# A four-layer graph network on one core: the kernel computes the issue order of its engines itself

## The chip, the cores and the metric

The kernel runs on one core of a Trainium2 chip. A core has five engines, each with its own queue of instructions that it works through in order: TensorE (PE in the profile; its weight loads are listed as PEld), VectorE (DVE), ScalarE (ACT), GpSimd (POOL) and SyncE (SP, which here only issues transfers). Engines wait for each other by semaphores. The metric is device time of one execution in microseconds. The page and the views come from one profiled execution; the times of the runs come from executions without the profiler.

## The reference

There are 16 graphs of 1024 nodes with 256 features, each with a dense 0/1 adjacency. Four layers follow each other, each on a normalized and rectified copy of x, and each adds its output to x:

```python
h = jnp.maximum(_layernorm(x), 0.0); x = x + layer0(h, adj)
# layer 0: e = leaky_relu(f1[i] + f2[j], 0.2), softmax over axis 1 where adj > 0, attention @ (h W), elu
# layer 1: the same, with softmax over the last axis
# layer 2: relu(x W_upd + (adj^T (x W_msg)) / degree + bias)
# layer 3: four heads of 64 features, leaky_relu with 0.01, softmax, relu(attention @ h + bias) + h,
#          then a layernorm over each head's 64 features with gamma and beta
```

All data are fp32, and the products are computed in fp32 (layer 2's message product in two fp32r halves, hi and lo).

## The kernel before

The 1024 nodes of a graph are eight tiles of 128. For each graph, `graph(b)` (a Python generator) traces: a `Norm` (statistics, normalization on ACT into `hn`, L671, transposition on TensorE into `pt_h`, L684, copy to `ht`, L685), then the four layers. A layer projects the eight tiles (`project`, L690), turns one projected column into a row that lies on all 128 partitions (`spread` writes `d_row` to HBM, L709; `everywhere` reads it back to every partition as `row`, L715), builds eight tiles of unnormalized weights `p` of 128 x 1024 on DVE (layer 0 L800 and L802, layer 1 L861, layer 3 L968, once per head) and multiplies them with the projected features on TensorE (L790, L854, L981; layer 2 multiplies the adjacency itself, L922, after its update product, L916). `residual` (L759, L760) adds the output to x on DVE and starts the next layer's `Norm`.

Layer 3's products (L981) are half as wide as the others: two matmuls of 64 columns each use the two halves of the array (`128*64` in the profile); all others use `128*128`. A matmul of fp32 is two records in the profile.

Graphs overlap. Each generator yields a number after each piece, a planned duration, and a small queue at the end of `tile_simple_stack` always resumes the generator with the earliest planned time; the next graph starts 120 planned microseconds after the one before. So the traced order interleaves layer 3 of a graph with layers 0 and 1 of the next. The traced order is not the issued one: the Tile scheduler takes the traced instructions, simulates them, and puts each engine's queue in the order in which they became ready, the earlier traced first. It also gives each tile one of its pool's slots. A tile's `tag` names its pool of slots and `bufs` their number: `p` has 8, `p3` (layer 3's `p`) 5, `hn` 3, and `e`, `v` and the PSUM tags `tr`, `mm`, `at` and `hd` 2.

`later = tc.keep_in_program_order` pins an instruction behind the one traced before it on its engine. The kernel before uses it for all transfers of SP, for the last DVE instructions of `tail` and for layer 0's early products. POOL issues the loads of x (L547) and of the adjacency's blocks (`load_adj`, L589), and computes the inverse deviations (`inv_std`, L596 and L597).

Of the kernel before, what the change touches and what calls it, by code (L numbers as in the profile page):

```python
# [14 lines left out]
P = 128  # L15
# [404 lines left out]

@with_exitstack
def tile_simple_stack(
# [35 lines left out]
    later = tc.keep_in_program_order  # L458
# [29 lines left out]
    def load_w(src, width, name, total, wait=True):  # L488
        t = const.tile([P, DC, total], F32, name=name)
        if wait:  # L490
            behind(t[:1, 0, :1])
        later(nc.sync.dma_start(t[:, :, :width], src.rearrange("(c p) f -> p c f", p=P)))
        return t
# [3 lines left out]
    def weights01(layer, w, w_t, a, order, wait=True):  # L497

        wx[layer] = t = load_w(w, D, f"wx{layer}", D + 2, wait)
        wts = work.tile([P, N], F32, tag="p3", name="wts", bufs=5)[:, : DC * D].rearrange("p (c f) -> p c f", c=DC)  # L500
        if wait:
            behind(wts[:1, 0, :1])
        later(nc.sync.dma_start(wts, w_t.rearrange("(c p) f -> p c f", p=P)))
        avs = small.tile([P, DC, 2], F32, tag="avs", name="avs", bufs=1)
        later(nc.sync.dma_start(avs, a.rearrange("(c p) k -> p c k", p=P)))
        for fc in range(DC):
            ps = mm_ps.tile([P, HALF], F32, tag="mm", name="ps_wa")
            for ec in range(DC):
                nc.tensor.matmul(
                    ps[:, :2], wts[:, ec, fc * P : (fc + 1) * P], avs[:, ec, :], start=(ec == 0), stop=(ec == DC - 1)  # L510
                )
            for k, to in enumerate(order):
                nc.vector.tensor_copy(t[:, fc, D + to : D + to + 1], ps[:, k : k + 1])

    def weights2():
        wx[2] = t = load_w(w2_msg, D, "wx2", 2 * D)
        later(nc.sync.dma_start(t[:, :, D:], w2_upd.rearrange("(c p) f -> p c f", p=P)))
        for name, src in (("bias2", bias2), ("bias3", bias3), ("gamma3", gamma3), ("beta3", beta3)):
            rows[name] = const.tile([P, D], F32, name=f"row_{name}")
            behind(rows[name][:1, :1])  # L520
            later(nc.sync.dma_start(rows[name], src.partition_broadcast(P)))
# [3 lines left out]
    def weights3():  # L525

        wx[3] = t = load_w(w3, D, "wx3", W3)
        w3ts = work.tile([P, N], F32, tag="p3", name="w3ts", bufs=5)[:HO, :].rearrange("p (h f) -> p h f", h=H)
        behind(w3ts[:1, 0, :1])
        later(nc.sync.dma_start(w3ts, w3_t))  # L530
        a3s = work.tile([P, D], F32, tag="e", name="a3s")[:HO, : H * T2].rearrange("p (h t) -> p h t", h=H)
        later(nc.sync.dma_start(a3s, a3))
        for fc in range(DC):
            for h in range(H):
                ps = mm_ps.tile([P, HALF], F32, tag="mm", name="ps_wa3")
# [4 lines left out]
    def load_x(b):  # L540
        t = state.tile([P, NT, D], F32, tag="xs", name="xs", bufs=3)
# [8 lines left out]
    class Mask:  # L550
# [10 lines left out]
        def load(self):  # L561
# [5 lines left out]
            raw = work.tile([P, HALF], I32, tag="raw", name="raw", bufs=self.AHEAD)  # L567
            later(nc.sync.dma_start(raw, adj_t[self.b, n * P : (n + 1) * P, g * HALF : (g + 1) * HALF]))
            self.raws.append((s, n, g, raw))

        def step(self, count=1):
            if self.bytes is None:
                self.bytes = state.tile([P, NT, N], U8, tag="mask", name="mask")
# [10 lines left out]
    def load_adj(b, g):  # L584

        t = state.tile([P, NT, EIGHTH], F32R, tag="adj", name="adj", bufs=4)
# [6 lines left out]
    def inv_std(var, n, scale, eps):  # L593

        rs = small.tile([P, NT * H], F32, tag="rstd", name="rs", bufs=6)
# [4 lines left out]
    def new_ht():  # L600
        return state.tile([P, DC, N], F32, tag="ht", name="ht", bufs=2)

    class Norm:
# [6 lines left out]
        def __init__(self, times=None):  # L610
            self.ht, self.rs, self.power, self.waiting, self.times, self.due = new_ht(), [], [], None, times, None
            if times is not None:
                self.shifts = small.tile([P, NT], F32, tag="shifts", name="shifts", bufs=2)
                self.scales = small.tile([P, 2, NT], F32, tag="scales", name="scales", bufs=2)
            self.mv = small.tile([P, NT, 2], F32, tag="mv", name="mv", bufs=4)
# [9 lines left out]
        def pair(self, xs, g, sums=None):  # L625

            if self.times is None:
                self.flip()
                shift = small.tile([P, 2], F32, tag="shift", name="shift")
            else:  # L630
                shift = self.shifts[:, 2 * g : 2 * g + 2]
            if sums is None:
                for k in range(2 * g, 2 * g + 2):
                    st = small.tile([P, 6], F32, tag="bn", name="st")
# [32 lines left out]
        def shifted(self, xs, g, by):  # L667
            hns = []
            for k, (scale, bias) in enumerate(by):
                hn = work.tile([P, D], F32, tag="hn", name="hn", bufs=3)  # L670
# [4 lines left out]
        def flip(self):  # L675
# [5 lines left out]
            pt = tr_ps.tile([P, DC, 2 * P], F32, tag="tr", name="pt_h")  # L681
# [5 lines left out]
    def project(norm, w, n, width):  # L687
        ps = mm_ps.tile([P, HALF], F32, tag="mm", name="ps_proj")
# [4 lines left out]
    def new_hs(name="hs"):  # L693
        return state.tile([P, NT, W3], F32, tag="hs", name=name, bufs=3)

    def spread(col, n, scales, name):
# [5 lines left out]
        ps = tr_ps.tile([P, P], F32, tag="tr", name="ps_col")  # L702
        nc.tensor.transpose(ps[:k, :], col, ident)
        all_rows = []
        for scale in scales:
            e = small.tile([H * NT, P], F32, tag="e_row", name="e_row", bufs=2)
            nc.scalar.activation(e[:k, :], ps[:k, :], AF.Exp, scale=scale)
            d = dram.tile([n, N], F32, tag=f"row_{name}", name="d_row", bufs=4)
            later(nc.sync.dma_start(d.rearrange("r (t p) -> (r t) p", p=P), e[:k, :]))  # L709
# [3 lines left out]
    def everywhere(d, tag):  # L713
        row = work.tile([P, N], F32, tag=tag, name="row", bufs=2)
        later(nc.sync.dma_start(row, d.partition_broadcast(P)))  # L715
        return row

    class Row:


        def __init__(self):
            self.ps = [hd_ps.tile([P, HALF], F32, tag="hd", name="ps_row") for _ in range(NHALF)]

        def add(self, n, f):
            g, k = divmod(n, PER)
            diag = work.tile([P, D], F32, tag="e", name="diag")[:, :P]
# [3 lines left out]
        def rows(self, scales):  # L730
            made = [work.tile([P, N], F32, tag="row", name="row", bufs=2) for _ in scales]
# [5 lines left out]
    def column(src, n):  # L737

        col = small.tile([P, H, NT], F32, tag="col", name="col", bufs=2)
# [7 lines left out]
    def weights(name):  # L747
        return work.tile([P, N], F32, tag="p", name=name, bufs=NT)

    def residual(xs, i, v, after, e=None):  # L750

        x = xs[:, i, :]
        if i % 2 == 0:
# [3 lines left out]
            after.sums = small.tile([P, 2], F32, tag="sums", name="sums")  # L757
# [7 lines left out]
    def layer0(b, xs, m, norm, after):  # L765
# [14 lines left out]
        q = small.tile([P, NT], F32, tag="q", name="q")  # L780
# [4 lines left out]
        early = [at_ps.tile([P, HALF], F32, tag="at", name="ps_o0") for _ in range(EARLY)]  # L785
        if b == 0:
            early += [hd_ps.tile([P, HALF], F32, tag="hd", name="ps_o0") for _ in range(NHALF)]

        def product(ps, i, j):
            m = nc.tensor.matmul(  # L790
                ps[:, :D], ps_[j][:, i * P : (i + 1) * P], hs[:, j, :D], start=(j == 0), stop=(j == NT - 1)
            )
            if i < len(early) and j < 7:
                later(m)

        for j in range(NT):
# [4 lines left out]
            z = small.tile([P, 2], F32, tag="z", name="z", bufs=8)  # L801
# [12 lines left out]
        for i in range(NT):  # L814
            if i < len(early):
                ps = early[i]
            else:
                ps = at_ps.tile([P, HALF], F32, tag="at", name="ps_o0")
                for j in range(NT):
                    product(ps, i, j)  # L820
            e = work.tile([P, D], F32, tag="e", name="e")
            nc.scalar.activation(e, ps[:, :D], AF.Exp)  # L822
            v = work.tile([P, D], F32, tag="v", name="v")
# [5 lines left out]
    def layer1(b, xs, mask, norm, after):  # L829
# [14 lines left out]
        q = small.tile([P, NT], F32, tag="q", name="q")  # L844
# [4 lines left out]
        early = [at_ps.tile([P, HALF], F32, tag="at", name="ps_o1") for _ in range(EARLY)]  # L849
        if b == 0:  # L850
            early += [hd_ps.tile([P, HALF], F32, tag="hd", name="ps_o1") for _ in range(NHALF)]
# [14 lines left out]
        for i in range(NT):  # L866
            if i < len(early):
                ps = early[i]
            else:
                ps = at_ps.tile([P, HALF], F32, tag="at", name="ps_o1")  # L870
# [5 lines left out]
            e = work.tile([P, D], F32, tag="e", name="e")  # L876
            nc.scalar.activation(e, ps[:, :D], AF.Exp, scale=z)
            v = work.tile([P, D], F32, tag="v", name="v")
# [5 lines left out]
    def degrees(b):  # L884

        t = small.tile([P, NT], F32, tag="deg", name="deg", bufs=2)
# [4 lines left out]
    def layer2(b, xs, norm, after):  # L891
# [6 lines left out]
        z = small.tile([P, NT], F32, tag="z2", name="z2", bufs=2)  # L898
        nc.vector.reciprocal(z, norm.times)
        hi = state.tile([P, NT, W3], F32R, tag="hs", name="hi", bufs=3)  # L900
        lo = state.tile([P, NT, W3], F32R, tag="hs", name="lo", bufs=3)
# [3 lines left out]
        for n in range(NT):  # L905
# [3 lines left out]
            rest = work.tile([P, D], F32, tag="e", name="rest")  # L909
# [3 lines left out]
        for j in range(NT):  # L913
            ps = hd_ps.tile([P, HALF], F32, tag="hd", name="ps_o2")
# [14 lines left out]
            v = work.tile([P, D], F32, tag="v", name="v")  # L929
# [7 lines left out]
    def layer3(b, xs, mask, norm, res):  # L937
# [20 lines left out]
        q = small.tile([P, NT, H], F32, tag="q3", name="q3", bufs=2)  # L958
        nc.scalar.activation(q, terms[:, :, H:], AF.Exp, scale=1.0 - S3)
        yield 9.44  # L960
        for h in range(H):
            next_row = everywhere(d_row[h + 1], "row3") if h + 1 < H else None
            pss = [hd_ps.tile([P, HALF], F32, tag="hd", name="ps_o3") for _ in range(NHALF)]
            for j in range(0, NT, run):
                ps_ = []
                for jj in range(j, j + run):
                    p = work.tile([P, N], F32, tag="p3", name="p3", bufs=5)
# [25 lines left out]
    def tail(b, xs, hs, res):  # L993
# [4 lines left out]
        for g in range(NHALF):  # L998
# [3 lines left out]
            m = small.tile([P, 2, PER * H], F32, tag="m3", name="m3", bufs=2)  # L1002
# [11 lines left out]
            sq = work.tile([P, N], F32, tag="p3", name="sq", bufs=5).rearrange("p (k e) -> p k e", e=HO)  # L1014
# [11 lines left out]
        for g, (t, o, of, m, sq) in enumerate(halves):  # L1026
            r = rs[g][:, : PER * H].unsqueeze(2).to_broadcast([P, PER * H, HO])
            if g == 0:

                later(nc.vector.tensor_tensor(of, of, along("gamma3"), op=OP.mult))  # L1030
                yield STEP
                of1 = halves[1][2]
                later(nc.vector.tensor_tensor(of1, of1, along("gamma3"), op=OP.mult))
                yield STEP
            later(nc.vector.tensor_tensor(o, o, r, op=OP.mult))
            yield STEP
            later(nc.vector.tensor_tensor(of, of, along("beta3"), op=OP.add))
# [3 lines left out]
            later(nc.vector.tensor_tensor(xv, of, xv, op=OP.add))  # L1041
            later(nc.sync.dma_start(out[b, g * HALF : (g + 1) * HALF].rearrange("(n p) d -> p n d", p=P), x))
            yield STEP

    def graph(b):
# [16 lines left out]
        res = state.tile([P, NT, H, HW], F32, tag="res", name="res", bufs=1)  # L1062
# [37 lines left out]
    bad = small.tile([P, 4], F32, tag="bad", name="bad")  # L1100
    t = work.tile([P, D], F32, tag="e", name="t_bad")[:, : B * NT]
# [10 lines left out]
    one = small.tile([P, 1], F32, tag="one", name="one")  # L1112
    nc.vector.memset(one, 1.0)
    ps = tr_ps.tile([P, P], F32, tag="tr", name="ps_bad")
    nc.tensor.matmul(ps[:1, :4], one, bad, start=True, stop=True)
    n_bad = small.tile([1, 1], F32, tag="n_bad", name="n_bad")
    nc.vector.tensor_reduce(n_bad, ps[:1, :4], axis=AX.X, op=OP.add)
    nc.vector.tensor_copy(flag, n_bad)

# [59 lines left out]
```

## Time and profile before

| | us |
|---|---|
| median of 3 runs | 2611.06 (2607.14 to 2614.94) |
| the profiled execution | 2612.95 |
| its span, first to last instruction | 2611.1 |
| TensorE busy | 2462.2 |
| DVE busy | 1978.2 |
| ACT busy | 1431.3 |
| POOL busy | 449.9 |
| granted TensorE clock, mean over the span | 0.987 |

In the profile a row of the groups names the line, the engine, the operation, what it writes and reads, the count, the busy time in us, the mean of one in ns, and the idle time of the engine just before with what ended it. The chain follows the execution back from its last instruction, at each step to what released it. In the timeline a row has the start, the duration, the engine, the line, the tiles and the count, and in brackets the idle time before it.

### The profile page before, as it was taken

To read this page: it belongs to the slowest core of one execution; us is meant where nothing else is said; L and a number is where in the kernel's file an instruction comes from. 1 tells how busy PE (TensorE), PEld (TensorE's weight loads), DVE (VectorE), ACT (ScalarE), POOL (GpSimd) and SP (SyncE) were. 2 spreads that over 40 slices of the span, in tenths; PEclk is the share of its full clock that TensorE was granted. 3 is DMA by queue.
4 is the path that set the end of the run, shared out by engine and by line. 5 is a ranking of instruction groups with operands and counts; after the bars stand their busy time and mean duration, and the time that the engine had idled before them with its cause. 6 is when DMAs were issued, how large, how long until landed. Compare 5 with 4: busy or idle time off the path is not lost.

```text
span 2611.1 us, 63088 instructions
## 1 busy us (share of the span) xinstructions
PE 2462.2 (94%) x26224; PEld 2102.5 (81%) x26224; DVE 1978.2 (76%) x3862; ACT 1431.3 (55%) x4036; POOL 449.9 (17%) x454
## 2 busy tenths in 40 slices
PE   6999999999999999999999999999999999999975
PEld 4788887888888888887888878888887888878864
DVE  6458778687777878778687777878768697777858
ACT  3763755637475563755637465563755637465350
POOL 1020211203021120211203021120211203011021
PEclk8999999999999999999999999999999999999987
DMA  4541522625225151522615224261522515224021
GB/s 136 111 85 55 141 54 78 130 66 131 62 89 103 62 134 55 134 58 80 132 59 137 63 86 105 63 134 55 134 58 80 133 57 138 64 67 103 25 65 36
DMA packets 212152, 232.17 MB, mean 89 GB/s; under 512 B 10344, under 2 KB 160976, under 8 KB 211856
## 3 DMA queue, kind: packets, MB, share of 16 engines
q1 hardware_dynamic: 74128, 144.14, 17.6%
q0 software_dynamic: 137728, 83.90, 17.2%
q8 instruction: 208, 3.41, 0.5%
q14 instruction: 88, 0.72, 0.1%
HBM read 210.78 MB, written 17.22 MB: 87 GB/s over the span
## 4 chain that ended last, share of the span: by engine, by line
PE 57%; DVE 17%; DMA 11%; ACT 10%; issue 3%; POOL 2%; SPq 0%; DVEq 0%; POOLq 0%; ACTq 0%
PE ps_o L790 16%; PE ps_proj L690 12%; PE ps_o L981 10%; DVE p L968 6%; PE ps_o L922 6%; PE ps_o L854 5%; DMA row<-d_row 5%; PE pt_h L684 5%; DVE p L861 4%; DMA raw<-in_adj_t 4%; PE ps_o L916 3%; ACT mask L581 2%; DMA d_row<-e_row 2%; ACT hn L671 2%; ACT unread L644 2%
## 5 line engine op out<-in xcount | busy, mean ns | idle before, releaser
L968 DVE SCALAR_TENSOR_TENSOR p<-row,q,mask 128x1024 f32<-128x1024 f32 x512 | 632.3, 1280 | 66.9 <-PE ps_o L981 55.7
L981 PEld LDWEIGHTS ps_o<-hb,p 128*64 128x64 f32 x16384 | 505.4, 138 | 101.8 <-DVE p L968 40.3
L981 PE MATMUL ps_o<-hb,p 128*64 128x65 f32 x16384 | 541.7, 224 | 28.7 <-DVE p L968 18.6
L690 PE MATMUL ps_proj<-wx,ht 128*128 128x258 f32 (+2 forms) x2048 | 509.8, 388 | 3.5 <-ACT hs L770 2.3
L790 PE MATMUL ps_o<-hs,p 128*128 128x256 f32 x2048 | 493.3, 386 | 18.8 <-ACT hs L804 18.8
L854 PE MATMUL ps_o<-hs,p 128*128 128x257 f32 x2048 | 496.9, 389 | 8.6 <-DVE p L861 8.6
L790 PEld LDWEIGHTS ps_o<-hs,p 128*128 128x128 f32 x2048 | 379.5, 191 | 75.0 <-ACT hs L804 23.2
L690 PEld LDWEIGHTS ps_proj<-wx,ht 128*128 128x128 f32 x2048 | 366.2, 191 | 77.2 <-ACT hs L770 9.7
L854 PEld LDWEIGHTS ps_o<-hs,p 128*128 128x128 f32 x2048 | 375.3, 191 | 62.9 <-DVE p L861 10.3
L596 POOL TENSOR_SCALAR rs<-mv 128x4 f32<-128x4 f32 (+1 forms) x112 | 41.2, 367 | 1557.4 <-ACT unread L644 1537.6
L597 POOL TENSOR_TENSOR rs<-rs,neg_half 128x4 f32<-128x4 f32 (+2 forms) x144 | 261.7, 1818 | 11.8
L759 DVE SCALAR_TENSOR_TENSOR xs<-e,xs 128x256 f32<-128x256 f32 x256 | 108.0, 422 | 180.7 <-ACT e L822 133.4
L671 ACT ACTIVATE hn<-xs,shift 128x256 f32<-128x256 f32 x384 | 175.2, 502 | 124.9 <-DVE shift L639 118.3
L684 PE MATMUL pt_h<-ident,hn 128*128 128x128 f32 x1024 | 181.8, 289 | 42.8 <-ACT hn L671 41.8
L922 PE MATMUL ps_o<-hi,adj 128*128 128x258 f32 x1024 | 203.2, 321 | 1.6
L684 PEld LDWEIGHTS pt_h<-ident,hn 128*128 128x128 f32 x1024 | 115.7, 142 | 110.0 <-ACT hn L671 93.2
L589 POOL DMA_DIRECT2D adj<-in_adj x128 | 114.5, 895 | 479.5 <-PE ps_o L922 477.9
L581 ACT ACTIVATE mask<-raw 128x512 uint8<-128x512 int32 x240 | 150.1, 626 | 69.7 <-DMA raw<-in_adj_t 42.8
L760 DVE SCALAR_TENSOR_TENSOR xs<-v,xs 128x256 f32<-128x256 f32 x384 | 161.4, 423 | 29.4 <-ACT v L824 16.5
L800 DVE SCALAR_TENSOR_TENSOR p<-row,q 128x1024 f32<-128x1024 f32 x128 | 161.8, 1274 | 18.5 <-DMA row<-d_row 16.9
L989 ACT ACTIVATE res<-ps_o 128x260 f32<-128x260 f32 x128 | 46.4, 374 | 232.4 <-PE ps_o L981 232.1
L922 PEld LDWEIGHTS ps_o<-hi,adj 128*128 128x128 f32 x1024 | 152.5, 190 | 14.2 <-ACT hi L908 4.8
(115 smaller groups left out, 3035.9 us busy)
## 6 DMA issues: line engine op xcount, KB each, us to landing
raw<-in_adj_t SPq DMA_DIRECT2D x256, 256.0 KB
adj<-in_adj POOLq DMA_DIRECT2D x128, 512.0 KB, 4.8
row<-d_row SPq DMA_DIRECT2D x109, 512.0 KB
xs<-in_x POOLq DMA_DIRECT2D x32, 512.0 KB, 7.1
out<-xs SPq DMA_DIRECT2D x32, 512.0 KB
wx<-in_w SPq DMA_DIRECT2D x3, 256.0 KB
d_row<-e_row SPq DMA_DIRECT2D x45, 4.0 KB
wts<-in_w_t SPq DMA_DIRECT2D x2, 256.0 KB
```

Source lines behind the costliest of these rows:

```text
L581: nc.scalar.activation(to, raw, AF.Square, accum_out=total)
L597: nc.gpsimd.tensor_tensor(rs[:, :n], rs[:, :n], neg_half[:, :n], op=OP.pow)
L671: nc.scalar.activation(hn, xs[:, 2 * g + k, :], AF.Relu, scale=scale, bias=bias)
L684: nc.tensor.transpose(pt[:, c, k * P : (k + 1) * P], hn[:, c * P : (c + 1) * P], ident)
L690: nc.tensor.matmul(ps[:, :width], norm.ht[:, c, n * P : (n + 1) * P], w[:, c, :width], start=(c == 0), stop=(c == DC - 1))
L760: nc.vector.scalar_tensor_tensor(x, v, 0.0, x, op0=OP.max, op1=OP.add, accum_out=after.sums[:, i % 2 : i % 2 + 1])
L790: m = nc.tensor.matmul(ps[:, :D], ps_[j][:, i * P : (i + 1) * P], hs[:, j, :D], start=(j == 0), stop=(j == NT - 1))
L800: nc.vector.scalar_tensor_tensor(p, row_a, q[:, j : j + 1], row_b, op0=OP.mult, op1=OP.max)
L854: nc.tensor.matmul(ps[:, : D + 1], ps_[j][:, i * P : (i + 1) * P], hs[:, j, : D + 1], start=(j == 0), stop=(j == NT - 1))
L922: nc.tensor.matmul(ps[:, : D + 2], adj_n[j][:, i, :], h[:, i, : D + 2], start=False, stop=(h is lo and i == NT - 1), skip_group_check=True,)
L968: nc.vector.scalar_tensor_tensor(p, row, q[:, jj, h : h + 1], mask[:, jj, :], op0=OP.max, op1=OP.mult)
L981: nc.tensor.matmul(pss[g][part, k * HW : (k + 1) * HW], ps_[t][:, i * P : (i + 1) * P][:, part], hbv[:, j + t, h, :], start=(j == 0 and t ...
```

## The change

A class `Order` is added, and its `run` is called after everything is traced. It reads the traced instructions with their operands, derives who must follow whom (overlapping reads and writes, PSUM tiles per engine, slots of tags), gives each instruction a duration of its own table, and makes a list schedule: the engine that can start earliest takes, of its ready instructions, the one of lowest rank. The rank is the sum of TensorE's durations before the instruction in traced order. The order found is pinned: each instruction gets an edge to the one before it on its engine, of the class NoSync, which sets the issue order and makes no semaphore. All uses of `later` go. `tile_of` replaces `pool.tile` and notes the number of slots of each tag. What is computed, and with which instructions, stays.

```diff
+class Order:
+    ENGINES = ("PE", "DVE", "Activation", "Pool", "SP")
+    SIGNAL = {"PE": 37.0, "DVE": 34.0, "Activation": 34.0, "Pool": 34.0, "SP": 25.0}
+    INTO_PE = 18.0
+    AFTER_WAIT = (104.0, 50.0)
+    LEAVE_HALVES, ENTER_HALVES = (102.0, 103.0), (93.0, 50.0)
+    STAY = 8000.0
...
+    def costs(self, k):
+        engine, op, acc = self.engine[k], str(self.ins[k].opcode), self.access[k]
+        size = [a[2][6] for a in acc]
+        most = max(size)
+        if op == "DMACopy":
+            total = 4.0 * size[0] * (acc[0][2][2] - acc[0][2][1])
+            return (60.0 if engine == "SP" else 950.0), 2000.0 + total / 220.0
+        if engine == "PE":
+            if any(a[2][0].startswith("ident") for a in acc):
+                return 110.0, 340.0
+            if any("float32r" in a[3] for a in acc):
+                return 121.0, 330.0
+            if acc[0][2][2] - acc[0][2][1] == 64:
+                return 57.0, 230.0
+            t = max(130.0, 2 * (size[0] * 2 / 2.4 + 2.5))
+            return t, t + 190.0
+        if engine == "DVE":
+            t = 75.0 if most < 40 else 62.0 + most / 0.9
+            return t, t + 88.0
+        if engine == "Pool":
+            t = 286.0 if op != "TensorTensor" else 450.0 + 160.0 * size[0]
+            return t, t - 80.0
+        reads = [a for a in acc if not a[1]]
+        t = 55.0 + 0.8 * max(size[0], size[-len(reads)])
+        t += 95.0 * (len(acc) > 2) + 44.0 * ("PSUM" not in reads[0][4]) + 95.0 * (len(acc) - len(reads) > 1)
+        return 1.04 * t, 1.04 * t + 110.0
...
+    def link(self, slots):
...
+        queue = [k for k in range(self.n) if self.engine[k] == "SP"]
+        self.behind = dict(zip(queue[1:], queue))
+
+    def seen(self, k, p):
+        if self.engine[p] == self.engine[k]:
+            if self.engine[k] == "PE":
+                return 0.0
+        return self.end[p] + self.SIGNAL[self.engine[p]] + (self.INTO_PE if self.engine[k] == "PE" else 0.0)
...
+    def run(self):
...
+        rank, at = [], 0.0
+        for k in range(n):
+            rank.append(at + k * 1e-4)
+            if self.engine[k] == "PE":
+                at += self.cost[k][0]
...
+        def offer(k):
+            for name in self.takes[k]:
+                tag = self.tag[name]
+                if not self.free[tag] or self.turn[tag][turn[tag]] != name:
+                    queue[tag].append(k)
+                    return
+            heapq.heappush(coming[self.engine[k]], (self.data(k), k))
...
+        for _ in range(n):
+            t, e = min(
+                (idle[e] if ready[e] else max(idle[e], coming[e][0][0]), e) for e in self.ENGINES if ready[e] or coming[e]
+            )
+            while coming[e] and coming[e][0][0] <= t:
+                k = heapq.heappop(coming[e])[1]
+                heapq.heappush(ready[e], (rank[k], k))
+            best = ready[e][0]
+            if e == "PE" and halves is False and self.halves[best[1]]:
+                other = min((r for r in ready[e] if not self.halves[r[1]]), default=None)
+                if other and other[0] - best[0] <= self.STAY:
+                    best = other
...
+            if e == "PE":
+                if halves is not None and halves != self.halves[k]:
+                    wait, late = self.LEAVE_HALVES if halves else self.ENTER_HALVES
+                    begin = max(due, idle[e] + wait)
+                elif due > idle[e]:
+                    late = self.AFTER_WAIT[self.halves[k]]
+                halves = self.halves[k]
...
+            if str(self.ins[k].opcode) == "DMACopy":
+                name = self.access[k][0][2][0][:3]
+                begin = max(begin + busy, pipe.get(name, 0.0))
+                pipe[name] = begin + lasts - 2000.0
...
+        for e in self.ENGINES:
+            for a, b in zip(order[e], order[e][1:]):
+                self.tc.add_manual_dep(
+                    self.ins[b], self.ins[a].name,
+                    mybir.DependencyInfo(mybir.DependencyClass.NoSync, mybir.DependencyReason.DATA), reason="order",
+                )
...
-    later = tc.keep_in_program_order
+    slots = {}
+
+    def tile_of(pool, shape, dtype, tag, name, bufs):
+        t = pool.tile(shape, dtype, tag=tag, name=name, bufs=bufs)
+        slots[t.tensor.tag] = bufs
+        return t
...
-        later(nc.sync.dma_start(row, d.partition_broadcast(P)))
+        nc.sync.dma_start(row, d.partition_broadcast(P))
...
-            if i < len(early) and j < 7:
-                later(m)
...
+    Order(tc, slots).run()
```

A duration of the table is a pair: how long the engine is taken, and when the result is there. `SIGNAL` is added from an instruction's end to whoever waits for it. `begin` and `late` are what TensorE loses at a change between half-width and full-width work or after a wait. `turn` holds, for each tag, its tiles in traced order: a tile's first instruction is offered only when the tile's turn has come and a slot is free.

## The prediction

> **What bounds the kernel now.** I read the page first (busy time and the 40 slices), then the groups by line, then the chain of waits in order of time for one period, then the timeline of TensorE alone, the waits of TensorE, and last the busy time by windows of one period.
>
> ```profile
> span 2611.1 us, 63088 instructions
> PE 2462.2 (94%) x26224; PEld 2102.5 (81%) x26224; DVE 1978.2 (76%) x3862; ACT 1431.3 (55%) x4036; POOL 449.9 (17%) x454
> PE   6999999999999999999999999999999999999975
> DVE  6458778687777878778687777878768697777858
> ```
>
> TensorE is at 9 tenths in every slice but the first and the last two, DVE at 4 to 9. So the bound is TensorE, and an order of instructions can only win what TensorE does not spend on products. How much that is, the 94% does not say, as a matmul that starts late behind another still counts as busy. The chain gives the pace of an undisturbed run (start, duration, what; L790 returns once per graph):
>
> ```profile
> 1297.97 6.91 PE ps_o L790 x32
> 1305.55 2.02 PE ps_o L981 x64
> 1313.43 3.88 PE ps_o L981 x128
> 1414.66 1.92 PE ps_o L922 x16
> 1454.99 6.91 PE ps_o L790 x32
> ```
>
> A full fp32 matmul record costs 6.91/32 = 0.216 us, one of the half-width matmuls of layer 3 (3.88 - 2.02)/64 = 0.0291, one of layer 2 1.92/16 = 0.120; six transposes start 0.65 us before what follows them (1372.01 to 1372.66 below), 0.108 each. By the counts of the groups: 16384 x 0.0291 = 477; L690, L790 and L854 with 2048 each and L916 with 512, 6656 x 0.216 = 1438; L922, 2048 x 0.120 = 246; L684, 1024 x 0.108 = 111; some 110 small ones, about 15. The floor is 2287 us, 142.9 per graph. The period is 1454.99 - 1297.97 = 157.0, so 14.1 us of each are lost, 212 in 15 periods. The rest of 2611 - 2287 = 324 is 7.4 before the first matmul, 29.3 after the last (at 2581.8), and 75 in the start and in the last graph, which has no other to overlap with.
>
> Now the 14.1. First, **switching**. TensorE alone in order of time:
>
> ```profile
> 1305.48 2.09 PE L981 MATMUL ps_o<-hb,p 128*64 128x65 f32 x64
> 1307.50 0.70 PE L790 MATMUL ps_o<-hs,p 128*128 128x256 f32 x2
> 1308.13 2.09 PE L981 MATMUL ps_o<-hb,p 128*64 128x65 f32 x64
> ```
>
> From 1305.48 to 1308.13 are 2.65 us; the work in it is 64 x 0.0291 + 2 x 0.216 = 2.29. No wait is marked, so going into half-width matmuls and out again costs 0.36. Counted in that timeline, TensorE does so 14 times in the period (210 times in the run): 14 x 0.36 = 5.0 us. Second, **idle**: the windows give TensorE 151.9 busy of 157.0, 5.1 idle. Third, 14.1 - 5.0 - 5.1 = 4.0 us in **short waits** that the overlap of matmuls hides from the busy time, mostly weight loads that wait for the second of two operands (in the waits, the weight load of pt_h waits 93.2 us for hn).
>
> Is the idle time one of order? One of the longest waits of this period:
>
> ```profile
> 1372.01 0.82 PE L684 MATMUL pt_h<-ident,hn 128*128 128x128 f32 x6
> 1372.66 3.20 PE L854 MATMUL ps_o<-hs,p 128*128 128x257 f32 x14
> 1376.36 1.30 ACT L671 ACTIVATE hn<-xs,shift 128x256 f32<-128x256 f32 x3
> 1376.91 0.44 PE L684 MATMUL pt_h<-ident,hn 128*128 128x128 f32 x2 [1.05 <-ACT hn L671]
> 1377.19 0.60 PE L854 MATMUL ps_o<-hs,p 128*128 128x257 f32 x2
> 1378.06 3.63 PE L854 MATMUL ps_o<-hs,p 128*128 128x257 f32 x16
> ```
>
> TensorE idles 1.05 us for hn while the L854 products right behind need nothing that is late (their p were made before 1363). The whole-run waits say that this kind is the largest, and that the others are for hs and p:
>
> ```profile
> PE pt_h L684 <- ACT hn L671: 41.8, 38, 3.8
> PE ps_o L790 <- ACT hs L804: 18.8, 17, 6.6
> PE ps_o L981 <- DVE p L968: 18.6, 24, 6.8
> ```
>
> But a part is no matter of order: DVE has nothing to spare in 40 us of each period (columns: length, then busy PE, PEld, DVE, ACT, POOL):
>
> ```profile
> 1337.00:1357.00 20.00, 17.39 (x324) 14.61 (x320) 18.74 (x18) 1.61 (x4) 0.00 (x0) 1.00 0.25 78
> 1357.00:1377.00 20.00, 18.95 (x203) 16.13 (x199) 19.15 (x47) 15.42 (x45) 0.73 (x2) 1.00 0.34 107
> ```
>
> The 2.6 us that TensorE idles from 1337 to 1357 stand against a DVE that is 94% busy with p.
>
> **The change, part by part.** No instruction is added or removed, no semaphore; each engine gets its same instructions in another fixed order. So every term is a difference of waits.
>
> *The durations of the plan.* Half-width 57 ns per instruction (two records, 58 by the chain), full 2 x (256 x 2/2.4 + 2.5) = 432 (two records, 432), layer 2's 121 (120), transposes 110 (108), entering and leaving halves 143 + 205 = 348 (0.36): they fit. DVE at 1024 columns 62 + 1024/0.9 = 1200; two L968 take 2.39 in the chain: fits. POOL's power at 4 columns 450 + 160 x 4 = 1090 against a mean of 1468 in the group of L597: 0.4 short. A row of 512 KB, 2000 + 524288/220 = 4383 ns, against 4.58 and 5.79 in the chain (at 1334.69 and 1402.83): up to 1.4 short. The present order is that of the Tile scheduler, whose durations the profile doesn't show; that they are off, only waits like the one above show.
>
> *Switching (STAY).* When TensorE is in full-width work and a half-width matmul is next, it stays with full-width work that is less than 8 us later in rank. Nothing kept back is worth 0.36 until DVE runs out of p3's five slots: L968 waits 55.7 us in all for L981 now, and would wait more. Bounds: no burst fewer, and, as five slots hold two pairs, 8 bursts for 16 pairs, 6 x 0.36 = 2.2. The row at 1313.43 (x128) shows that two pairs do merge; I take 4 bursts fewer, 1.4 us per period.
>
> *Idle.* Bounds 0 and 5.1. I leave the 2.6 of the DVE-bound window and take nearly all of the other 2.5: 2.3.
>
> *Short waits.* Bounds 0 and 4.0. The plan counts 34 + 18 ns from an end on ACT or DVE to TensorE, and may put full products between two transposes, but each switch of stream makes new ones: nearly half, 1.8.
>
> *Against it: rows that land later than planned.* Three rows per graph gate a stage (two of layer 0 issued together count as one, one of layer 1, the first of layer 3). DVE's queue is in order, so behind a p that waits stand the residuals (L759, L760), the shift (L639) and so hn and TensorE's transposes. Between 0 and 3 x 1.4 = 4.2 us per period, if TensorE had nothing else; DVE waits for rows now 16.9 (L800) + 9.9 (L968) + 4.6 (L861) in the run, 2 per period, and TensorE mostly has products in stock. Nearer to 0: 0.5 lost. The short power on POOL goes with it: DVE's scales (L661) wait 33.3 us for it in 32 times already, 0.4 more each is under 1 us per period for DVE, and it lies beside TensorE's products.
>
> The DMA share in the window from 1397 to 1417 is 0.81, at 206 GB/s, and the row of 5.79 us falls into it, while that of 4.58 falls where the share is 0.08 to 0.25. The Trainium skill, "DMA: Bandwidth & Descriptors", section "Issuing engines are not separate DMA queues", says that transfers of all issuers run on the same 16 DMA engines and interleave. The plan gives each kind of tile a pipe of its own, so the rule speaks against it: by the plan the term would be 0 and the time 2523, by the rule, with TensorE paying all of 4.2, 15 x 3.7 = 56 more than I forecast, about 2587.
>
> *Queues and taken-out pins.* SP's transfers were kept in traced order and still are (`behind`): 0, covered by the same waits as now. POOL's adj loads (L589) wait 477.9 us for L922, and an rs (L597) that is put behind one of them waits too; POOL is 17% busy, and the plan times both: 0, and if one rs per graph were caught, its 1.5 us delay hn, within the 4.2 above. The pins on the tail's DVE instructions and on layer 0's early products are replaced by rank: 0.
>
> *Sum.* Per period 1.4 + 2.3 + 1.8 - 0.5 = 5.0, 75 us in 15. The start and the last graph are bound by landings and by DVE (from 2547 to 2580, 28 L968 fill 33.57 us): 5 gained, bounds -10 and 25. 2611.1 - 80 = 2531. The profiled execution took 2612.95 with what lies around its span, the median of the runs is 2611.06, so nothing is added: **2531 us**.
>
> **Rivals.** *More is won.* DVE's order is planned too, so p might be ahead where it is short now. All upper ends, (2.2 + 5.1 + 4.0) x 15 + 25 = 195, give 2416; without the DVE-bound 2.6 x 15 = 39 it is 2455. Against: no greedy order fills everything.
>
> *Less is won.* TensorE's gains outside the DVE-bound 40 us are given back there, as TensorE arrives earlier at the same p. Only switching and some short waits remain, 1.4 + 0.8 per period: 2611 - 33 = 2578. For it: DVE at 19.15 of 20. Against: over the period DVE is busy 122 of 157.
>
> *The order comes out as it was.* Both are greedy by traced order, so the pins could repeat it: 2611. Against: the 0.36 per switch and the wait at 1376 are things that the present order plainly ignores.
>
> *Slower: slots in traced order.* The plan hands the slots of a tag out in the order of tracing (`turn`): tr, mm, at, hd, e and v with two slots, hn with three, shared by two graphs. A graph whose hn is late then holds back the other's tiles of the same tag, and the real run, which drifts from the plan, pays it on TensorE. Price: one more wait as long as the longest for hn, 3.8 us, in each period, 57 us; with switching gained and nothing else, 2611 + 57 - 21 = 2647. It decides from 5 us per period if all else is as forecast, from 1.4 if only switching is won. For it: hn is the largest wait already. Against: the plan counts these waits and fills them.
>
> **Chances.** Forecast (2490 to 2575) 0.45, more 0.12, less (2575 to 2603) 0.15, as it was 0.06, slower 0.22. A measurement of this kernel tells 0.3%, 8 us, from no change, so faster 0.72, same 0.06, slower 0.22. The forecast's own range is 2490 to 2575. For 8 in 10 I go down to the 2455 worked out above and up to 2640, which takes in most of the slower case.
>
> **What would show it.** Right: the period between two L790 x32 rows at 152, fewer than 12 bursts of L981 per period, the wait of pt_h for hn under 20 us in the run, TensorE at 96% or more. Switching wrong: 13 or more bursts, or L968 waiting over 100 us for L981. Rows: L800 waiting for row over 30 us. Slots: waits of hn, e or v for TensorE or DVE that are not there now, and a period over 157. The forecast is wrong as a whole if the period is not under 155.

## The result, and the profile after

The changed kernel takes 2635.39 us (median of 4 runs, 2629.23 to 2638.74); the kernel before took 2610.38 beside it (4 runs). The ratio is 1.0092, interval 1.0067 to 1.0116: 0.9% slower, where 3% faster was forecast. The profiled execution has a span of 2627.3 us at a granted clock of 0.976; before it was 2611.1 at 0.987.

First the head of the page of the changed kernel:

```profile
span 2627.3 us, 63105 instructions
PE 2455.4 (93%) x26224; PEld 2132.3 (81%) x26224; DVE 1967.3 (75%) x3862; ACT 1428.1 (54%) x4036; POOL 452.4 (17%) x454
```

TensorE's busy time fell by 7 us (2462.2 to 2455.4), but the span rose by 16, so its time without a matmul rose from 148.9 to 171.9. The lines have new numbers: L790 is L1018 now, L981 is L1207, L968 is L1194, L922 is L1148, L671 is L899, L684 is L912, L581 (the mask) is L809, L568 (its load) is L796, L888 (`deg`) is L1114. The chain of waits in order of time (start, duration, what) gives the period again, with a long transfer in it:

```profile
1308.33 6.91 PE ps_o L1018 x32
...
1410.57 6.59 DMA raw<-in_adj_t
1417.19 0.73 ACT mask L809 x2
1417.94 0.18 DVE deg L1114
1418.35 0.39 DVE lo L1137
...
1466.18 6.91 PE ps_o L1018 x32
...
1625.85 6.91 PE ps_o L1018 x32
```

The two periods shown are 157.85 and 159.67 us (1466.18 - 1308.33 and 1625.85 - 1466.18), against 157.0 before and 152 forecast. The end of what sets the time runs through a load of the next graph's adjacency (`raw`), its mask on ACT, `deg` and then `lo` on DVE. The waits of the whole run (engine, line, what for: total, times, longest) say the same:

```profile
PE ps_o L1148 <- DVE lo L1137: 38.4, 14, 3.7
PE ps_o L1207 <- DVE p L1194: 25.1, 34, 6.2
...
PE pt_h L912 <- ACT hn L899: 11.0, 6, 5.5
...
DVE deg L1114 <- ACT mask L809: 60.5, 15, 5.2
...
DVE p L1194 <- PE ps_o L1207: 17.9, 28, 0.8
...
ACT mask L809 <- DMA raw<-in_adj_t: 54.2, 31, 4.0
```

Two things went as forecast: the wait of the transposes for hn is 11.0 us (41.8 before; "under 20"), and p waits 17.9 us for TensorE (55.7 before), so longer bursts didn't starve it. Two rows are new: the waits of the kernel before list none of TensorE for `lo` and none of `deg`. Both come about once per graph (14 and 15 times). The timeline of one such place (start, busy time of the group, engine, line; in brackets the idle time ahead of it and what ended that):

```profile
1409.14 0.90 SPq L943 DMA_DIRECT2D row<-d_row  x2
1410.13 0.39 SPq L1268 DMA_DIRECT2D out<-xs  x1
1410.57 0.50 SPq L796 DMA_DIRECT2D raw<-in_adj_t  x1
...
1417.19 0.63 ACT L809 ACTIVATE mask<-raw 128x512 uint8<-128x512 int32 x1 [2.81 <-DMA raw<-in_adj_t]
...
1417.82 0.46 ACT L1136 ACTIVATE rest<-ps_proj,z 128x256 f32<-128x256 f32 x1
1417.94 0.17 DVE L1114 TENSOR_TENSOR deg<-squares 128x8 f32<-128x8 f32 x1 [3.98 <-ACT mask L809]
...
1418.30 0.43 DVE L1137 TENSOR_TENSOR lo<-rest,hi 128x256 fp32r<-128x256 f32 x1
...
1418.79 0.87 PE L1148 MATMUL ps_o<-lo,adj 128*128 128x258 f32 x5 [2.52 <-DVE lo L1137]
...
1420.27 2.07 PE L1142 MATMUL ps_o<-wx,ht 128*128 128x256 f32 x4 [0.61 <-ACT edges L1157]
```

Read it upwards from the row at 1418.79. TensorE stands for 2.52 us and needs the next `lo` of layer 2. `lo` needs `rest`, which in ACT's fixed order comes behind the mask of the next graph. DVE could not have run `lo` either: its fixed order has `deg` of the next graph first, and that needs the same mask. The mask waits for `raw`, issued on SP's queue behind two `row` transfers of 512 KB and a store (1.4 us after the first of them), and landing 6.59 us after its issue. Nothing of this graph needs that mask.

In the kernel before, masks waited for `raw` too, and the same burst stands on SP's queue (waits of the run, then the timeline):

```profile
ACT mask L581 <- DMA raw<-in_adj_t: 42.8, 59, 2.1
...
1402.38 0.82 SPq L715 DMA_DIRECT2D row<-d_row  x2
1403.30 0.39 SPq L1042 DMA_DIRECT2D out<-xs  x1
1403.78 0.46 SPq L568 DMA_DIRECT2D raw<-in_adj_t  x1
...
1410.58 0.63 ACT L581 ACTIVATE mask<-raw 128x512 uint8<-128x512 int32 x1 [0.57 <-DMA raw<-in_adj_t]
```

That `raw` is as late, 6.8 us from issue to mask, but ACT stands for it only 0.57 us, and nothing that TensorE waits for is held up by this mask.

The stretch of layer 2 around it, by windows (columns: length, then busy PE, PEld, DVE, ACT, POOL, then granted clock, DMA share, GB/s):

```profile
1403.00:1423.00 20.00, 15.66 (x78) 12.53 (x77) 8.19 (x21) 12.59 (x36) 3.37 (x4) 0.93 0.52 142
```

4.3 us of 20 are idle, and the clock is 0.93.

Counting changes into half-width work over all matmul rows in order of time gives 151 bursts after and 211 before: 4 fewer per period, as forecast. So the switching was saved, and the time went elsewhere.

### The profile page after: what moved, and what is told of

Read it like the earlier page. It is cut to its first block, busy times and chain, and to the rows that moved or that the text cites. A ratio compares the mean times of both kernels' runs of the same rounds, so it can differ in the third digit from the quotient of the medians.

```text
span 2627.3 us, 63105 instructions
## 1 busy us (share of the span) xinstructions
PE 2455.4 (93%) x26224; PEld 2132.3 (81%) x26224; DVE 1967.3 (75%) x3862; ACT 1428.1 (54%) x4036; POOL 452.4 (17%) x454
## 3 DMA queue, kind: packets, MB, share of 16 engines
q8 instruction: 208, 3.41, 0.5%
## 4 chain that ended last, share of the span: by engine, by line
PE 69%; DVE 12%; ACT 7%; DMA 7%; issue 3%; POOL 1%; SPq 0%; DVEq 0%; POOLq 0%; ACTq 0%
PE ps_o L1018 16%; PE ps_o L1080 13%; PE ps_o L1207 13%; PE ps_proj L918 11%; PE ps_o L1148 8%; DMA raw<-in_adj_t 6%; DVE p L1194 5%; DVE p L1087 5%; PE ps_o L1142 4%; PE pt_h L912 3%; ACT hn L899 2%; ACT mask L809 1%; ACT ht L913 1%; DMA d_row<-e_row 1%; ACT hs L998 1%
## 5 line engine op out<-in xcount | busy, mean ns | idle before, releaser
L1194 DVE SCALAR_TENSOR_TENSOR p<-row,q,mask 128x1024 f32<-128x1024 f32 x512 | 629.2, 1278 | 25.4 <-PE ps_o L1207 17.9
L1207 PEld LDWEIGHTS ps_o<-hb,p 128*64 128x64 f32 x16384 | 501.1, 138 | 91.8 <-issue 50.3
L1207 PE MATMUL ps_o<-hb,p 128*64 128x65 f32 x16384 | 528.9, 224 | 36.3 <-DVE p L1194 25.1
L918 PE MATMUL ps_proj<-wx,ht 128*128 128x258 f32 (+2 forms) x2048 | 521.3, 388 | 14.1 <-ACT rest L1136 11.4
L1018 PE MATMUL ps_o<-hs,p 128*128 128x256 f32 x2048 | 484.2, 382 | 8.3 <-ACT hs L1030 8.3
L1080 PE MATMUL ps_o<-hs,p 128*128 128x257 f32 x2048 | 485.2, 387 | 0.9 <-DVE p L1087 0.6
L1018 PEld LDWEIGHTS ps_o<-hs,p 128*128 128x128 f32 x2048 | 380.4, 192 | 57.2 <-ACT hs L1030 9.3
L899 ACT ACTIVATE hn<-xs,shift 128x256 f32<-128x256 f32 x384 | 175.8, 503 | 136.3 <-DVE shift L867 115.7
L1148 PE MATMUL ps_o<-hi,adj 128*128 128x258 f32 x1024 | 229.5, 343 | 6.6 <-ACT hi L1134 6.5
L1148 PE MATMUL ps_o<-lo,adj 128*128 128x258 f32 x1024 | 167.7, 300 | 38.4 <-DVE lo L1137 38.4
L809 ACT ACTIVATE mask<-raw 128x512 uint8<-128x512 int32 x240 | 150.3, 630 | 80.7 <-DMA raw<-in_adj_t 54.2
L1148 PEld LDWEIGHTS ps_o<-hi,adj 128*128 128x128 f32 x1024 | 167.1, 203 | 29.7 <-ACT hi L1134 17.2
L913 ACT COPY ht<-pt_h 128x512 f32<-128x512 f32 x256 | 144.8, 584 | 78.3 <-PE pt_h L912 75.8
L912 PE MATMUL pt_h<-ident,hn 128*128 128x128 f32 x1024 | 174.2, 280 | 13.1 <-ACT hn L899 11.0
L1148 PEld LDWEIGHTS ps_o<-lo,adj 128*128 128x128 f32 x1024 | 144.9, 199 | 42.8 <-DVE lo L1137 41.3
```

The costliest lines, as they stand in the source:

```text
L809: nc.scalar.activation(to, raw, AF.Square, accum_out=total)
L899: nc.scalar.activation(hn, xs[:, 2 * g + k, :], AF.Relu, scale=scale, bias=bias)
L912: nc.tensor.transpose(pt[:, c, k * P : (k + 1) * P], hn[:, c * P : (c + 1) * P], ident)
L913: nc.scalar.copy(self.ht[:, :, g * 2 * P : (g + 1) * 2 * P], pt)
L918: nc.tensor.matmul(ps[:, :width], norm.ht[:, c, n * P : (n + 1) * P], w[:, c, :width], start=(c == 0), stop=(c == DC - 1))
L1018: nc.tensor.matmul(ps[:, :D], ps_[j][:, i * P : (i + 1) * P], hs[:, j, :D], start=(j == 0), stop=(j == NT - 1))
```

## The experiments

The theory after reading the result ("A"): the plan's clock for transfers is wrong. In it each kind of tile has a pipe of its own, so `raw` never queues behind `row` or the store, and lands 2000 + 262144/220 = 3192 ns after its issue; the chain shows 6.59 us. Believing that, the plan places mask and `deg` early in two in-order queues, ahead of what TensorE needs. The rival is the one forecast: the slots in traced order. Ratios are to the kernel before, run on the same chip beside each.

**One planned pipe per issuing engine (e5).**

```diff
-                name = self.access[k][0][2][0][:3]
+                name = e
```

> One line of the plan is changed: transfers are planned one after another per issuing engine (SP, POOL) in place of one pipe per kind of tile. Theory A, late transfers: the plan lets row, out and raw move side by side, on the chip the raw behind them lands about 3 us late, mask (ACT) and deg (DVE) wait for it in their in-order queues, and rest, lo and TensorE's L1148 behind them; that is 5 us of each period and most of what is lost. Then the waits of deg for mask (60.5 us) and of L1148 for lo (38.4) fall under 10, the period from 159 to 153 or 154 us, and the time to 2520 to 2560. Theory B, slots handed out in traced order: the transfers' times don't matter, within 15 us of the changed kernel (2620 to 2650).

Measured 2534.16 us, ratio 0.9714 (0.9691 to 0.9738). One line, which changes nothing but the plan's idea of when transfers land, is worth 1.0092 - 0.9714 = 3.8%, 99 us. The slots are handed out by the same rule as before, so the slots theory, by which the transfers' times don't matter, falls. A second measurement on another chip (e5_again):

> e5_pipe_engine once more, beside these three on one chip: 2525 to 2545.

2533.53 us, 0.9705 (0.9678 to 0.9732): it repeats. The head of e5's page:

```profile
span 2531.0 us, 63106 instructions
PE 2422.3 (96%) x26224; PEld 2107.5 (83%) x26224; DVE 1964.9 (78%) x3862; ACT 1428.1 (56%) x4036; POOL 453.4 (18%) x454
```

Its chain in order of time:

```profile
1103.48 6.91 PE ps_o L1018 x32
...
1255.76 6.91 PE ps_o L1018 x32
```

The period is 152.28. Its waits for TensorE and for the mask:

```profile
PE ps_o L1207 <- DVE p L1194: 24.6, 33, 6.1
...
PE pt_h L912 <- ACT hn L899: 6.5, 3, 3.2
PE ps_o L1148 <- ACT hi L1134: 3.3, 15, 0.3
...
ACT mask L809 <- DMA raw<-in_adj_t: 5.2, 6, 1.5
```

The wait for `lo` is gone, `deg` waits for nothing, and the mask waits 5.2 us in the whole run instead of 54.2. Its window of layer 2:

```profile
1345.00:1365.00 20.00, 19.47 (x104) 15.96 (x103) 9.52 (x24) 16.41 (x47) 3.30 (x4) 1.00 0.55 161
```

TensorE is busy 19.47 of 20 us there, at full clock.

**One pipe for everything (e1):** the same line with `name = "all"`.

> As the run before, but all transfers, POOL's too, share one planned pipe. Theory A: also 2520 to 2560; better than one pipe per engine only if SP's and POOL's transfers really share, worse if not. Theory B: 2620 to 2650.

2536.97 us, 0.9722 (0.9701 to 0.9744): the same as e5 within the intervals. Whether POOL's loads share the pipe doesn't matter; that SP's share one does.

**No staying in full-width work (e3):** the changed kernel with `STAY = 0.0`.

> The changed kernel with STAY = 0: TensorE no longer stays with full-width work. Theory A with the gain from switching as forecast: bursts of L1207 back from about 150 to about 200, some 50 x 0.36 = 18 us more, 2645 to 2660; the layer 2 wait for lo stays at about 38 us. Theory C, that holding half-width work back starves DVE and layer 3 and is the loss: 2590 to 2615.

2646.67 us, 1.0146 (1.0122 to 1.0169). Staying is worth 0.54%, 14 us, in the kernel as changed (by the two intervals, 5 to 23). It also shows that the stall isn't tied to one victim; here TensorE waits in the same place for `hi`, behind the same mask (the waits of e3):

```profile
PE ps_o L1148 <- ACT hi L1134: 65.9, 15, 5.7
```

**The same in e5 (e6):** `name = e` and `STAY = 0.0`.

> One planned pipe per issuing engine as in e5_pipe_engine, and STAY = 0. If a switch saved is worth 0.36 us to the whole, as the prediction had it, 60 bursts more cost 21 us against e5_pipe_engine: about 2555. If what staying saves on switches is given back elsewhere (p3's slots full, DVE waiting for L1207), within 8 us of e5_pipe_engine: 2530 to 2542.

2551.21 us, 0.9779 (0.9753 to 0.9806), with 211 bursts where e5 has 151: 0.0065 x 2608 = 17 us for 60 bursts, 0.28 us each (forecast 0.36). The two intervals allow 8 to 26 us, 0.13 to 0.43 each.

**Only `deg` held back (e4):** the changed kernel, where `deg` on DVE follows the last `lo` traced before it.

```diff
         self.behind = dict(zip(queue[1:], queue))
+        last = None
+        for k in range(self.n):
+            if self.engine[k] == "DVE":
+                name = self.access[k][0][2][0]
+                if name.startswith("deg") and last is not None:
+                    self.before[k].add(last)
+                if name.startswith("lo"):
+                    last = k
```

> The changed kernel with one more edge in the plan: deg waits in DVE's order behind the last lo traced before it. Theory A says that two queues are stopped by the same late raw, ACT at mask (with rest behind it) and DVE at deg: taking deg out of the way leaves lo waiting for rest, so the wait of deg falls under 10 us but L1148 still waits 30 us or more for lo, and the time stays at 2620 to 2640. If DVE's queue alone carried the loss: 2575 to 2605.

2640.40 us, 1.0122 (1.0101 to 1.0144): nothing won. The wait of `deg` is gone from the waits, that of TensorE is not:

```profile
PE ps_o L1156 <- DVE lo L1145: 39.7, 14, 3.8
```

ACT's queue alone is enough: the mask still stands ahead of `rest` there.

**Both held back (e7):** `deg` behind the last `lo` on DVE, and every mask on ACT behind the last `rest` traced before it; the pipes stay wrong.

```diff
+            if name[:3] in last and self.engine[k] in ("DVE", "Activation") and last[name[:3]] is not None:
+                self.before[k].add(last[name[:3]])
+            if name.startswith("lo"):
+                last["deg"] = k
+            if name.startswith("rest"):
+                last["mas"] = k
```

> The changed kernel with its wrong pipes, but deg held behind the last lo traced before it (DVE) and each mask behind the last rest traced before it (ACT). Theory A, that the raws are planned too early and stop two in-order queues: with nothing of layer 2's lo behind them, L1148's wait for lo falls from 38 to under 10 us and the time to 2550 to 2600, though raws are as late as before. If the lateness acts in another way (rows for p, adjacency for L1148): 2620 to 2645.

2560.61 us, 0.9809 (0.9781 to 0.9837). With the wrong clock of transfers kept, two constraints bring back 1.0092 - 0.9809 = 2.8%, 74 of the 99 us. What is left shows in its waits, where the mask now stands ahead of the next thing that TensorE needs, `edges` on ACT:

```profile
PE ps_o L1151 <- ACT edges L1166: 25.9, 15, 2.9
...
ACT mask L818 <- DMA raw<-in_adj_t: 23.5, 21, 2.4
```

**Only `raw` planned late (e2):** the changed kernel, with 3500 ns added to the landing of each `raw`.

```diff
+            late = 3500.0 if acc[0][2][0].startswith("raw") else 0.0
-            return (60.0 if engine == "SP" else 950.0), 2000.0 + total / 220.0
+            return (60.0 if engine == "SP" else 950.0), 2000.0 + total / 220.0 + late
```

> The changed kernel with its pipes per kind of tile, but every raw planned to land 3.5 us later. Theory A, the raws alone: near e5_pipe_engine, 2535 to 2575. If the rows for p are as much to blame: 2580 to 2625.

2585.46 us, 0.9905 (0.9875 to 0.9936). The 2535 to 2575 of theory A was missed: `raw` alone gives about half (49 of 99 us). The time lies in the range that the other expectation had, rows being as much to blame; but DVE's waits for rows are 12.8 us in the run, against 7.1 in the changed kernel, so a direct wait for rows is not the missing half. The wait for `lo` is gone, and TensorE's waits show a new one, for the adjacency tiles that POOL loads:

```profile
PE ps_o L1149 <- DMA adj<-in_adj: 10.7, 13, 2.0
```

A fixed delay isn't a queue: it is wrong for each load that finds the queue empty, and the other transfers stay too early. What of the other half belongs to which of these was not taken apart.

**SP's issue time and a shorter STAY (e8, e9, e11).** An issue on SP takes 0.29 to 0.39 us in the changed kernel's trace (medians: `d_row` 0.29, `raw` 0.33, `row` 0.34, the store 0.39), and the plan has 60 ns. On top of e5: e8 has 330 ns and `STAY = 6000`, e11 only the 330 ns, e9 only `STAY = 6000`.

> e5_pipe_engine with an SP issue planned at 330 ns in place of 60 (the profile shows 320 to 390 ns for one) and STAY = 6000. If the plan still loses by transfers that are issued later than planned, 2515 to 2530; if what remains lies elsewhere, within 10 us of e5_pipe_engine (2525 to 2545).

> e5_pipe_engine with an SP issue planned at 330 ns alone: the other edit of e8_sp_issue. If planning the issue at its profiled length makes the greedy order worse by itself, 2550 to 2575; if not, 2525 to 2545.

> e5_pipe_engine with STAY = 6000 alone: the first of the two edits of e8_sp_issue. If the bound on staying was what e8 lost by, 2555 to 2570; if it is harmless, 2520 to 2545.

e8: 2565.87 us, 0.9834 (0.9805 to 0.9863); e11: 2554.0, 0.9787 (0.9771 to 0.9803); e9: 2525.78, 0.9674 (0.9658 to 0.969). So the truer issue time makes the order some 20 us worse (e11 against e5_again, on the same chip), which I had not expected, and the shorter STAY is not told apart from the longer one (e9 against e5_again, intervals that overlap). The waits of TensorE in e11:

```profile
PE ps_proj L918 <- ACT rest L1136: 9.1, 29, 0.4
PE ps_proj L918 <- ACT hs L1171: 6.0, 15, 0.4
```

No single large wait has come back; its period is 153.5. The loss is idle time: TensorE is 130.5 us without a matmul, against 108.7 in e5, and as long busy (2421.3 and 2422.3); the two rows above, 3.1 and 0.2 in e5, are part of it. Why the greedy schedule falls into this order stays open. It also says how finely such parts can be read: an edit of the plan that makes one number truer moves the order by 20 us, so the 49 and 74 of the 99 us are rough shares.

**e5 with both holds (e10).**

> One planned pipe per issuing engine and, with it, deg and mask held behind lo and rest. If lateness of raws still costs something with the right pipes, a few us below e5_pipe_engine, 2515 to 2530; if the pipes alone had removed it, the holds only constrain the order: 2530 to 2550.

2525.90 us, 0.968 (0.9664 to 0.9696). With e9 it is the fastest, 3.2 to 3.3% faster than the kernel before; the two are not told apart, and each is 0.25 to 0.3% ahead of e5 on the same chip, with intervals that overlap. Once the plan has a better idea of when `raw` lands, the holds are worth little.

## Why the prediction was wrong, point by point

**The step that failed** is "Against it: rows that land later than planned", with its "Nearer to 0: 0.5 lost" per period. The changed kernel against e5 measures the wrong pipes at 99 us, 6.6 per period, beyond my upper bound of 4.2. Had the term been 6.6, my own sum would have given 5.5 - 6.6 = -1.1 per period: 2611.1 + 17 - 5 = 2623, slower (measured 2635). Three things were missing in it:

- It priced only `row`, by way of DVE's p. That path lost nothing: DVE waits 7.1 us in the run for rows, where it waited 31.4 before. The same formula times `raw`, which SP issues right behind the rows and a store: 6.59 us measured, 3.19 planned, and it acts by way of ACT. In the kernel before, the mask already waited 42.8 us for `raw`; the prediction passes over this wait of an engine that is busy 55%.
- It took the lateness as something that TensorE's stock of products hides. But the plan decides *where* to put the consumer by the time it believes in. It put the next graph's mask and `deg`, which nobody needs for a long time, ahead of `rest` and `lo`, which TensorE needs at once. A load that is 3.4 us late then stops ACT and DVE together, and TensorE for 2.5. e4 shows that ACT's queue alone does it, and e7 that moving both behind is worth 74 us.
- The price of a wait was its length. TensorE also lost clock (last section): about 28 us in the run against the kernel before, 33 against e5.

The rule of the Trainium skill that I weighed ("DMA: Bandwidth & Descriptors", "Issuing engines are not separate DMA queues") was the right warning, and the 2587 that I worked out from it too little, since I applied it to `row` alone. The page says that transfers of all issuers interleave on 16 engines; here it was those of one issuer that mattered, as e1 (one pipe) and e5 (one per issuer) are equal.

**Switching: right.** 4 bursts fewer per period were forecast and 60 in the run counted. They are worth 14 us (after against e3) to 17 (e5 against e6); the forecast was 1.4 x 15 = 21. The 0.36 was read off one place; over all it is 0.23 to 0.28, and the intervals do not exclude 0.36.

**Idle and short waits: right, once the transfers are planned rightly.** In e5 TensorE's time without a matmul is 2531.0 - 2422.3 = 108.7 us, 40 less than before; forecast were 2.3 x 15 = 35. Its busy time is 40 us less; forecast were (1.4 + 1.8) x 15 = 48 of switching and short waits. The period is 152.28 against 152, and the time 2534 against 2531. The forecast fits this kernel and not the one that it was made for, whose plan has the wrong line in it. That the sizes agree so well is in part chance: the 0.5 for late rows, for example, is taken off in the forecast and not told apart in e5, and e11 lies 20 us off after an edit that should not hurt.

**The rivals.** "Slower: slots in traced order" came out near in time (2647 against 2635) and wrong in its cause: e5 keeps the slots. Of its signs the period over 157 is there, but no new kind of wait for hn, e or v is; the new waits are TensorE's for `lo` and that of `deg`. The 2635 also lies within the 2455 to 2640 given for 8 in 10, whose upper end was drawn to take in this rival: luck. "Less is won" fails in e5: TensorE's gains were not given back to DVE, whose p makes TensorE wait 24.6 us in the run, 6 more than the 18.6 before. "As it was" is excluded by the counts of bursts.

**What would have shown it in advance:** in the trace before, SP's queue issues two rows, a store and a `raw` within 1.9 us (1402.38 to 1404.24), the mask waits for that `raw` until 1410.58, 6.8 us after its issue, and the plan's table gives each kind its own pipe. The question to ask was which in-order engine would now wait for that landing, and who stands behind it. At another place of the same period this was already so: the wait of 1.05 us for hn at 1376.91, which the prediction reads as one of order between transposes and products, is reached in the chain through two loads of `raw` and the masks on ACT (start, duration, what):

```profile
1365.05 2.81 DMA raw<-in_adj_t
1367.89 1.40 ACT mask L581 x4
1369.30 3.61 DMA raw<-in_adj_t
1372.93 1.12 ACT mask L581 x3
...
1376.46 0.41 ACT hn L671
```

## What to carry to other kernels

One wrong entry in the resource model of a planned order can lose more than all its right ones win, here 99 us against the 75 by which e5 is ahead of the kernel before: model each issuing queue as one server before you tune durations by nanoseconds. Where in-order engines are pinned, an instruction that depends on a transfer and is needed late belongs behind what the bound engine needs now; e7 shows that such a rule saved about three quarters of the loss even with a wrong clock, and e11 that a truer clock doesn't by itself give a better greedy order. Look at the waits of engines that are far from busy: what waits there unnoticed is what a new order may put in front of the bound engine.

## What the runs showed of the hardware

**These waits of TensorE were paid nearly twice.** After the wait of 2.52 us that begins at 1416.3 the granted clock falls, and the work right behind it takes double: the four L1142 matmuls at 1420.27 take 2.07 us, where four such take 1.03 in the kernel before:

```profile
1409.29 1.03 PE L916 MATMUL ps_o<-wx,ht 128*128 128x256 f32 x4
```

By windows of the changed kernel (columns as above):

```profile
1414.00:1418.00 4.00, 1.94 (x14) 1.63 (x13) 0.06 (x1) 1.19 (x4) 0.83 (x1) 1.00 0.60 217
1418.00:1422.00 4.00, 2.60 (x10) 2.12 (x10) 3.97 (x11) 1.47 (x6) 2.19 (x3) 0.76 0.60 152
1422.00:1424.00 2.00, 2.00 (x12) 1.91 (x12) 2.00 (x2) 0.37 (x1) 0.35 (x1) 0.63 1.84 321
```

The clock records of the whole run show 19 stretches at half clock, 127 us together, against 9 and 71 us before and 6 and 61 us in e5. Between 100 us and 2400 us after the start there are 13 of them, 68 us, against one of 3.4 us in each of the other two. The 56 us more than before are 28 us of lost work, as much as 0.987 - 0.976 of the span. Against e5 it is 66 us more, 33 of lost work: a third of the 99. No wait in the profile names it; it hides in the busy time, which is 33 us higher than e5's, while the time without a matmul is 63 us higher.

Not each wait costs clock. Of the 14 waits for `lo`, 2.3 to 3.7 us long, 13 have a fall of the clock within 2 us of their end; of the 15 waits for `edges` in e7, 0.4 to 2.9 us long, 5 do.

The Trainium skill, "TensorE: Matmul & The Clock Gate", section "What's actually happening", tells of an activity window of 3413 ns that runs freely and sets the clock to half after an idle window. It agrees in kind: all 19 falls of the changed kernel lie on one grid of 3.413 us, and the stretches last 3.41, 6.83 and 10.24 us, but for one of 28.4 at the end. But here the window needn't be empty. In the 3.41 us up to the fall at 1420.09 TensorE was busy for a quarter, in none before a fall for more than 36%, and from the first fall on each window of that grid at full clock with 47% or more kept it. Over all the runs the highest share before a fall is 60% and the lowest that kept the clock 42%, so where the border lies is known only to that.

**Transfers of one queue were served nearly one after another.** The packets of the two rows ran from 1410.10 to 1414.65, the store's from 1413.98 to 1416.12 and those of `raw` from 1415.34 to 1416.73: the 256 KB took 1.4 us once their turn came, and had waited nearly 5 for it since the issue at 1410.57. A `raw` issued at 1396.41, half a microsecond behind another store but no rows, landed in 3.90.
